# Two transformer layers on one core: weight blocks made behind each tile's sums, shared slots for the heads' large buffers, and every load on SP's queue

## The chip, the cores and the metric

The kernel runs on one core of one Trainium2 chip. The metric is the device time of one execution in microseconds (us). A core has TensorE (PE, with its weight loads as PEld), VectorE (DVE), ScalarE (ACT), GpSimd (POOL) and SyncE (SP). Each takes its own instructions in order, and they wait for one another, and for DMA transfers, through semaphores. A DMA is issued by one engine's instruction stream: in this kernel by SP or by ACT. Line numbers (L1091) are those of the kernel before.

## The reference

Two pre-norm layers, each of an attention and a feed-forward network (FFN), on x of 4 batches, 512 tokens and 1024 channels, in float32:

```python
x = x + L0_attention(layernorm(x))   # across the 4 batches, per token and channel group
x = x + L0_ffn(layernorm(x))         # base product + two of eight routed low-rank experts
x = x + L1_attention(layernorm(x))   # 32 causal heads, latent keys and values, rotary part
x = x + L1_ffn(layernorm(x))

def L1_attention(x):
    q = rmsnorm(x @ wq_a.T, q_a_ln_w) @ wq_b.T          # 256 -> 32 heads x (64 + 64)
    ckv, k_pe = split(x @ wkv_a.T)                      # 64 latent + 64 rotary channels
    kv = rmsnorm(ckv, kv_a_ln_w) @ wkv_b.T              # per head: 64 for keys, 128 for values
    scores = (q_full . k_full) * scale, causal
    return (softmax(scores) @ v) @ wo.T

def L1_ffn(x):
    routing = softmax(x[:, 179:-1].mean(1) @ router_W.T + router_b)     # per batch
    return x @ W.T + b + 2 * sum_e routing[e] * (x @ A[e].T) @ B[e].T
```

## The kernel before

The tokens are 16 tiles of 128 rows. Products are kept near float32 accuracy by splitting each operand into a high and a low part of type fp32r: ACT copies the high part (`ah`, `cxh`), and POOL or DVE subtracts it from the source for the low part (`al`, `cxl`). Three matmuls per product follow (`matmul3`, L133 to L135). A tile framework decides the order of the instructions on each engine from dependencies and from when buffers of its pools come free; an engine then runs that list strictly in order. SP's queue is one such list.

The stages, with their place in the profiled span:

- **Layer-0 attention**, up to about 107 us.
- **Layer-0 FFN**, to about 370 us, tile by tile: base products (`base`), routing, `finish`, statistics. Between its steps the loop advances a generator, `prepare_w1` (L366). It forms the differences of blocks of the last FFN's weights, `t1` to `t4` beside the plain `b11`, `b22`, `b21`, in halves s = 0 and 1. These go to DRAM (`w1_d`).
- **Projections of the layer-1 attention**, to about 468 us. They leave the queries' latents and the keys in DRAM.
- **Heads**, to 1560.8 us. 32 heads in four groups of eight; in a group, four batches; in a batch, eight units (one head each). A unit has scores and softmax (L773, L776), transposes of the probabilities (`turn`, L797), and the context product (`psv`, L813). `load_batch` (L563) fetches the next batch's latent queries `qT` (1.05 MB) and keys, double buffered. `prepare_output` (L888) builds the group's output weights from `wo` and `wv` (loaded by `fetch_output` into a pool of its own) as Strassen-like blocks b and t. Behind the next batch's units runs `project` (L820 on) as a filler: seven products per pair of tiles (`poa`, `pob`), added to rows `xs` of x that are loaded from `x_d` and stored again.
- **Transition and last FFN**, to the end. The last projection, of group 3 and batch 3, runs after the last unit, to 1602.6. The last FFN works on eight pairs of tiles q. `norm` and `turn1` (L1069) normalise and transpose a pair's blocks. `operands` (L1085 on) forms the seven combinations and splits them (L1090 ACT, L1091 POOL). `product` does seven steps for two halves of columns s, each 12 matmuls of 128x288. The first pair runs its seven steps with s = 0 first and then with s = 1. `biased` (L1191) adds the bias to the rows `xo` (and `raw`) on POOL, `mixture` makes the routing of a batch. The second pair starts at 1654.9.

The loads of that stage: `load_w1` issues them on ACT's queue, four t blocks of 1.18 MB and three b blocks of 0.59 MB for each s. s = 0 goes out once the attention's pools are closed (L1107), s = 1 once the projection has ended (L1138). `split_w1` splits the b blocks. `fetch_h` loads a pair's rows for `norm`, `fetch_x` loads them again as `xo`.

```python
def load_w1(kind, s):
    w = w1[kind, s] = w1p[s].tile([P, 2, ND // 2, W1B], FR, name=f"w{kind}{s}")
    if kind[0] == "t":
        nc.scalar.dma_start(out=f32(w), in_=w1_d[kind, s])
    else:
        nc.scalar.dma_start(out=f32(w)[:, 1], in_=w1_d[kind, s][:, 0])
```

Of the kernel before, what the change touches and what calls it, by code (L numbers as in the profile page):

```python
# [9 lines left out]
F32 = mybir.dt.float32  # L10
# [35 lines left out]
def block_kernel(ctx: ExitStack, tc: tile.TileContext, a: dict, out: bass.AP):  # L46
# [319 lines left out]
    def prepare_w1(room, u):  # L366

        c, s = divmod(u, 2)
        b11, b12, b21, b22 = (room[:, k * W1B : (k + 1) * W1B] for k in range(4))
        for n, (kind, to, a0, a1) in enumerate((("t1", b11, b12, b11), ("t3", b12, b22, b12),  # L370
                                                ("t2", b22, b22, b11), ("t4", b21, b21, b22))):
            V.tensor_tensor(to, a0, a1, ALU.subtract)
            n = 4 + 2 * ((4 * u + n) % 3)
            h, l = (room[:, (n + k) * W1B : (n + k + 1) * W1B].bitcast(FR) for k in range(2))
            A.copy(h, to)
            G.tensor_tensor(l, to, f32(h), ALU.subtract)
            nc.sync.dma_start(
                out=w1_d[kind, s][:, :, c, :],
                in_=room[:, n * W1B : (n + 2) * W1B].rearrange("p (k n) -> p k n", k=2))
            if kind == "t4" and u + 1 < ND:  # L380
                fetch_w1(room, u + 1)
            yield

    attn = ExitStack()
    cc = attn.enter_context(tc.tile_pool(name="c_const", bufs=1))
# [16 lines left out]
    with tc.tile_pool(name="b_h", bufs=2) as hp, tc.tile_pool(name="b_hTh", bufs=2) as hTh, \  # L402
# [64 lines left out]
        for s, t in enumerate(order):  # L467
            prep = prepare_w1(room1, s - 2) if 0 <= s - 2 < ND else iter(())
# [6 lines left out]
            next(prep, None)  # L475
# [7 lines left out]
            next(prep, None)  # L483
# [5 lines left out]
            next(prep, None)  # L489
# [11 lines left out]
            next(prep, None)  # L501
            if s == ND + 2:
                rawA = raw()
                for ch in range(ND):
                    nc.sync.dma_start(out=rawA[:, ch * NA : (ch + 1) * NA], in_=a["waT"][ch])
                split_shared(cc, 0)
# [6 lines left out]
    k_d = [dram.tile([P, TPB, KVR], F32, name=f"k_d{b}") for b in range(NB)]  # L513
    wqp = attn.enter_context(tc.tile_pool(name="c_wq", bufs=2))
# [48 lines left out]
    def load_batch(b):  # L563
        q = inp.tile([P, 2, 2, S], FR, name="qT")
        nc.sync.dma_start(out=f32(q), in_=q_d[b])
        kT = inp.tile([P, 2, S], FR, name="kT")
        nc.sync.dma_start(out=f32(kT), in_=kT_d[b])
        kF = inp.tile([P, P], F32, name="kF")
        nc.sync.dma_start(out=kF, in_=kF_d[b])
        k = inp.tile([P, TPB, KVR], F32, name="k")  # L570
        nc.sync.dma_start(out=k, in_=k_d[b])
        return q, kT, kF, k
# [38 lines left out]
    with tc.tile_pool(name="c1_w", bufs=1, side="right") as wap, \  # L611
# [73 lines left out]
        for s in range(NT + 1):  # L685
# [4 lines left out]
            if s > 0:  # L690
                keep(s - 1, qk[s - 1])
                if order1[s - 1] == TPB - 1:
                    batches[0, 0] = load_batch(0)
# [12 lines left out]

    with ExitStack() as c2:
# [6 lines left out]
        wop = heads.enter_context(tc.tile_pool(name="c2_wo", bufs=2))  # L714
# [165 lines left out]
        def fetch_output(g, pr):  # L880
            wo = [wop.tile([VD, D], F32, name="wo") for k in range(2)]
            for k in range(2):
                nc.sync.dma_start(out=wo[k], in_=a["woT"][g * HG + 2 * pr + k])
            wv = wop.tile([VD, 2, KVR], F32, name="wv")
# [79 lines left out]

        filler = None
        cx = behind = None
        for u in range(NU + 3):
# [38 lines left out]
            if u < NU:  # L1006
                g, b, i = units[u]
                if i == 2 and u + HG < NU:
                    nx = units[u + HG]
                    batches[nx[:2]] = load_batch(nx[1])  # L1010
                if b == 0 and i == 0:
                    wo_raw = fetch_output(g, 0)
                if (b, i) in ((NB - 1, 0), (NB - 1, 4)) and g + 1 < NG:
                    wq_raw = fetch_query(2 * g + 2 + i // 4)
        heads.close()
# [7 lines left out]
        w1p = [dp.enter_context(tc.tile_pool(name="d_w0", bufs=1))]  # L1023
# [5 lines left out]
        w1, hs, blocks, sums, stats, xo = {}, {}, {}, {}, {}, {}  # L1029
        late = raw()  # L1030

        def load_w1(kind, s):
            w = w1[kind, s] = w1p[s].tile([P, 2, ND // 2, W1B], FR, name=f"w{kind}{s}")
            if kind[0] == "t":
                nc.scalar.dma_start(out=f32(w), in_=w1_d[kind, s])
            else:
                nc.scalar.dma_start(out=f32(w)[:, 1], in_=w1_d[kind, s][:, 0])

        def split_w1(kind, s, eng):
            w = w1[kind, s]  # L1040
            A.copy(w[:, 0], f32(w)[:, 1])
            eng.tensor_tensor(w[:, 1], f32(w)[:, 1], f32(w)[:, 0], ALU.subtract)

        def load_x(q, tiles):
            for t in range(2):
                for k in range(2):
                    nc.sync.dma_start(out=tiles[t][:, k * 512 : (k + 1) * 512], in_=x_d[2 * q + t][k])
# [10 lines left out]
        def norm(q, t):  # L1058
            s = 2 * q + t
            normalise(hs[q][t], hs[q][t], *stats[s][0], stats[s][1])  # L1060
# [46 lines left out]
        fetch_h(0)  # L1107
        LOADS = ("b11", "b22", "b21", "t1", "t2", "t3", "t4")
        for kind in LOADS:
            load_w1(kind, 0)  # L1110
        mv = small.tile([P, TPB, 2], F32, name="mv")
# [7 lines left out]
        fetch_x(0)  # L1119
        advance(filler, 4)  # L1120
        for k in range(3):
            split_w1(LOADS[k], 0, G)
            advance(filler, 2)
            if k < 2:
                turn1(0, k)
            advance(filler, 2)
        fetch_h(1)
# [8 lines left out]
    lop = dp.enter_context(tc.tile_pool(name="d_lo", bufs=2, space=PSUM))  # L1136
    bias1 = broadcast_rows(w1r, a["b1"], D, "bias1")
    for kind in LOADS:  # L1138
        load_w1(kind, 1)
# [5 lines left out]
    nc.sync.dma_start(out=late[:, 0:D], in_=a["b1T"])  # L1145
# [81 lines left out]
    for q in range(NP):  # L1227
        inputs[q] = wk.tile([P, 2, ER], F32, name="inputs")
        odd, more = q % 2, q + 1 < NP
        if q == 0:  # L1230
            for step in range(7):
                product(0, step, (0,))
                if step > 3:
                    split_w1(LOADS[step - 4], 1, V)
        for step in range(7):
# [19 lines left out]
            if step == 4 and q == 0:  # L1255
# [92 lines left out]
```

## Time and profile before

| What | Value |
|---|---|
| runs shown | 1869.5, 1864.55, 1866.59 us; median 1866.59 |
| the profiled execution | 1862.94 us, its span 1861.0 us |
| mean granted TensorE clock | 0.982 |
| busy: PE, DVE, ACT, POOL | 1739.8, 1368.1, 875.0, 913.6 us |
| moved by DMA | 225.72 MB, mean 121 GB/s |
| SP's queue (q1), ACT's (q10) | 210.80 MB, 12.98 MB |

The page cuts the span into 40 slices of 46.5 us and gives each engine's busy share in tenths (9 is 90 % or more), the granted clock of TensorE and the DMA engines' share. A line of waits reads "engine, result and line <- what ended the wait: us in total, times, longest". A timeline row reads start, duration, engine, line, operation, result <- operands, count, and in brackets the idle time before it and what ended it. Rows such as ACTq or SPq are DMA issues on that engine. Busy shares mean different things in different stages: the stages above are bounded by different engines, so each is read by itself.

### The profile page before, as it was taken

How to read it: one execution, taken by the hardware profiler on the slowest of the kernel's cores; microseconds unless marked ns; L12 is line 12 of the kernel's file. 1: busy time of each engine (PE TensorE's matmuls, PEld its weight loads, DVE VectorE, ACT ScalarE, POOL GpSimd, SP SyncE). 2: the span in 40 equal slices, each digit the busy share in tenths (PEclk: the TensorE clock that was granted, in tenths of full speed). 3: DMA queues.
4: the chain of work that ended last, by engine and by line, in shares of the span. 5: the costliest groups of instructions: out<-in, count | busy, mean ns of one | idle time of the engine just before them, and what ended most of it. 6: DMA issues, size and time to landing. Idle time of an engine off the chain costs nothing.

```text
span 1861.0 us, 30786 instructions
## 1 busy us (share of the span) xinstructions
PE 1739.8 (93%) x10280; PEld 1461.4 (79%) x10280; DVE 1368.1 (74%) x3534; ACT 875.0 (47%) x2272; POOL 913.6 (49%) x819
## 2 busy tenths in 40 slices
PE   6978999999989999989999999999999998589998
PEld 6977899999667777757777757777757776488998
DVE  6787765576787777688777688777688875487685
ACT  6332211165665556465556465556465654233222
POOL 0364211010666666566666566666566653564552
PEclk9988999999999999999999999999999999799999
DMA  7235300034533324443324343324334326712431
GB/s 257 80 128 189 132 35 35 35 97 137 175 108 107 125 92 135 126 134 120 126 91 137 126 133 120 126 91 136 118 116 141 103 64 224 299 60 100 134 116 46
DMA packets 130813, 225.72 MB, mean 121 GB/s; under 512 B 22176, under 2 KB 58016, under 8 KB 127584
## 3 DMA queue, kind: packets, MB, share of 16 engines
q1 hardware_dynamic: 128640, 210.80, 34.4%
q10 hardware_dynamic: 2016, 12.98, 1.7%
q8 instruction: 81, 1.33, 0.3%
q14 instruction: 76, 0.62, 0.1%
HBM read 156.60 MB, written 70.65 MB: 122 GB/s over the span
## 4 chain that ended last, share of the span: by engine, by line
PE 70%; DVE 9%; POOL 4%; DMA 3%; ACT 3%; issue 2%; SPq 0%; POOLq 0%; ACTq 0%; DVEq 0%
PE psv L813 7%; PE pst L797 6%; PE pss L133 3%; PE pss L135 3%; PE pss L134 3%; PE po L133 3%; PE po L135 3%; PE po L134 3%; PE pob L133 3%; PE poa L133 3%; PE psq L133 3%; PE acc L135 3%; PE psq L135 2%; PE acc L133 2%; PE psq L134 2%; PE acc L134 2%
## 5 line engine op out<-in xcount | busy, mean ns | idle before, releaser
L776 ACT ACTIVATE p<-p,mn 128x512 f32<-128x512 f32 (+3 forms) x512 | 284.1, 557 | 240.3 <-DVE mn L773 239.6
L598 POOL TENSOR_TENSOR qf<-qf,ropeT 64x512 f32<-64x512 f32 x128 | 167.7, 1310 | 205.5 <-ACT qf L594 204.3
L773 DVE CUSTOM_DVE_ANT_0 p<-pss,causal 128x512 f32<-128x512 f32 (+3 forms) x512 | 231.7, 487 | 23.3 <-PE pss L135 19.5
L797 PE MATMUL pst<-ident,p 128*128 128x128 f32 x1280 | 185.4, 274 | 4.6 <-DVE pT L799 4.3
L599 POOL TENSOR_TENSOR qf<-qf,t 64x512 f32<-64x512 f32 x128 | 165.2, 1290 | 46.5 <-DVE t L597 39.0
L797 PEld LDWEIGHTS pst<-ident,p 128*128 128x128 f32 x1280 | 153.6, 142 | 32.9 <-DVE pT L799 7.4
L799 ACT COPY pT<-pst 128x512 f32<-128x512 f32 x256 | 143.7, 578 | 63.4 <-PE pst L797 63.4
L813 PE MATMUL psv<-pT,k 128*64 128x384 f32 (+3 forms) x1024 | 164.7, 441 | 0.0
L133 PE MATMUL pss<-kT,ql 128*128 128x512 f32 (+2 forms) x384 | 143.8, 374 | 22.0 <-POOL ql L607 13.9
L607 POOL TENSOR_TENSOR ql<-qf,qh 128x384 fp32r<-128x384 f32 x128 | 132.8, 1037 | 59.4 <-DVE qh L606 54.9
L835 POOL TENSOR_TENSOR cxl<-s,cxh 128x256 fp32r<-128x256 f32 x128 | 95.1, 744 | 131.3 <-ACT cxh L834 124.7
L133 PE MATMUL po<-w_h,hTl 128*128 128x384 f32 (+1 forms) x384 | 135.5, 353 | 13.3 <-DVE x L333 13.3
L813 PEld LDWEIGHTS psv<-pT,k 128*64 128x64 f32 x1024 | 73.2, 137 | 86.7 <-issue 75.8
L134 PE MATMUL po<-w_l,hTh 128*128 128x384 f32 (+1 forms) x384 | 132.1, 344 | 0.0
L135 PE MATMUL po<-w_h,hTh 128*128 128x384 f32 (+1 forms) x384 | 131.9, 344 | 0.0
L135 PE MATMUL pss<-kT,qh 128*128 128x512 f32 (+2 forms) x384 | 130.9, 341 | 0.0
L134 PE MATMUL pss<-kT,qh 128*128 128x512 f32 (+2 forms) x384 | 130.4, 340 | 0.0
L799 DVE COPY pT<-pst 128x256 f32<-128x256 f32 x128 | 53.9, 421 | 78.7 <-PE pst L797 77.1
L133 PEld LDWEIGHTS pss<-kT,ql 128*128 128x128 f32 x384 | 72.5, 189 | 45.0 <-POOL ql L607 18.1
L594 ACT COPY qf<-psq 128x512 f32<-128x512 f32 x126 | 73.9, 586 | 65.1 <-PE psq L135 62.8
L133 PE MATMUL psq<-qT,wql 128*128 128x512 f32 x252 | 101.7, 403 | 1.5 <-DVE t L597 1.5
L596 DVE TENSOR_TENSOR t<-psq,ropeT 32x512 f32<-32x512 f32 x126 | 87.7, 696 | 19.9 <-ACT qf L594 15.6
(521 smaller groups left out, 4975.7 us busy)
## 6 DMA issues: line engine op xcount, KB each, us to landing
xs<-x_d SPq DMA_DIRECT2D x128, 256.0 KB
x_d<-xs SPq DMA_DIRECT2D x128, 256.0 KB
qT<-q_d SPq DMA_DIRECT2D x16, 1024.0 KB
wo<-in_woT_dram SPq DMA_DIRECT2D x32, 512.0 KB
rb<-r_d SPq DMA_DIRECT2D x128, 128.0 KB
w_t<-raw SPq DMA_DIRECT2D x32, 288.0 KB
wt<-w_t ACTq DMA_DIRECT2D x8, 1152.0 KB
x<-in_x_dram SPq DMA_DIRECT2D x16, 512.0 KB
```

The lines of the kernel that those rows point to most:

```text
L133: T.matmul(ps, lhsT=al, rhs=bh, start=start, stop=False, **kw)
L134: T.matmul(ps, lhsT=ah, rhs=bl, start=False, stop=False, **kw)
L135: T.matmul(ps, lhsT=ah, rhs=bh, start=False, stop=stop, **kw)
L598: G.tensor_tensor(f[mid], f[mid], ropeT[mid, 0, :], ALU.mult)
L599: G.tensor_tensor(f[mid], f[mid], t2[mid], ALU.add)
L607: G.tensor_tensor(l, f[:, P:S], f32(h), ALU.subtract)
L773: V.tensor_tensor_reduce(out=to, in0=ps[:, 0:n], in1=causal[:, S - n : S], scale=1.0, scalar=-NEG, op0=ALU.add, op1=ALU.min, accum_out=mn[ ...
L776: A.activation(to, to, AF.Exp, bias=mn[:, i : i + 1], scale=-1.0, accum_out=rs[:, i : i + 1])
L797: T.transpose(ps[:, w : w + P], p[:, OF[i] + j * P : OF[i] + (j + 1) * P], ident)
L799: copy(pT[:, AT[js[0]] : AT[js[0]] + w], ps[:, 0:w])
L813: T.matmul(ps[n * KVR : (n + 1) * KVR, S - w : S], lhsT=k[:, j, :], rhs=pTs[u + n][:, AT[j] : AT[j] + w], start=(j == 0), stop=(j == TPB - 1))
L835: G.tensor_tensor(l, src, f32(h), ALU.subtract)
```

## The change

1. `prepare_w1` is a plain function. It is called once for each tile, after its `finish`, stores and statistics, and no longer a quarter at a time between the tile's products. The pool of the shared constants (`c_const`) opens after that stage.
2. Two slots, A and B, of 9216 bytes per partition each hold the latent queries and the keys of a batch, in turn by batch. A slot C holds one pair's `wo` and `wv`, in place of the pool `wop`. All three outlive the heads.
3. In the last batch of the last group the slots take weights of the last FFN: t1 into A (unit 4), t2 into C (unit 5), both s = 0. t3 later goes into B. The rows `xo` of the first pair and the transposed bias are asked for in unit 1 of that batch. The first pair is normalised from `xo[0]`, and `fetch_h(0)` is gone.
4. All loads of the weights go through SP's queue. The order of the loads for s = 1 is b11, b22, b21, t1, the bias, the router, t2, the second pair's rows, t3, t4.
5. `biased(0)` and the split of the transposed bias move from step 4 to step 6 of the first pair. The splits of b blocks alternate between POOL and DVE, and b21 of s = 0 is split after the first step.

The core of the diff:

```diff
@@ layer-0 FFN
-            prep = prepare_w1(room1, s - 2) if 0 <= s - 2 < ND else iter(())
...
-            next(prep, None)
+            if 0 <= s - 2 < ND:
+                prepare_w1(room1, s - 2)
@@ heads
+    slots = [ctx.enter_context(tc.tile_pool(name="slots", bufs=1))] * 2
...
+    def slot(k):
+        return slots[k].tile([P, ND * W1B], F32, name="slot" + "ABC"[k])
+
+    def load_batch(g, b):
+        room = slot((g * NB + b) % 2)
+        n = 4 * S
+        q = room[:, 0:n].bitcast(FR).rearrange("p (k c s) -> p k c s", k=2, c=2)
...
+        k = room[:, n : n + TPB * KVR].rearrange("p (j d) -> p j d", j=TPB)
...
         def fetch_output(g, pr):
-            wo = [wop.tile([VD, D], F32, name="wo") for k in range(2)]
+            room = slot(2)
+            wo = [room[:, k * D : (k + 1) * D] for k in range(2)]
...
+                if (g, b) == (NG - 1, NB - 1) and i == 1:
+                    late = raw()
+                    xo[0] = [late[:, (t + 1) * D : (t + 2) * D] for t in range(2)]
+                    load_x(0, xo[0])
+                    nc.sync.dma_start(out=late[:, 0:D], in_=a["b1T"])
+                if (g, b) == (NG - 1, NB - 1) and i in (4, 5):
+                    load_w1("t" + "12"[i - 4], 0, (0, 2)[i - 4])
@@ transition and last FFN
-                nc.scalar.dma_start(out=f32(w), in_=w1_d[kind, s])
+                nc.sync.dma_start(out=f32(w), in_=w1_d[kind, s])
...
-            normalise(hs[q][t], hs[q][t], *stats[s][0], stats[s][1])
+            normalise(hs[q][t], hs[q][t] if q else xo[0][t], *stats[s][0], stats[s][1])
...
-        fetch_h(0)
-        for kind in LOADS:
+        for kind in LOADS[:3]:
             load_w1(kind, 0)
...
-            split_w1(LOADS[k], 0, G)
+                split_w1(LOADS[k], 0, (G, V)[k])
...
+            if k:
+                load_w1("t" + "34"[k - 1], 0, (1, None)[k - 1])
...
-    for kind in LOADS:
-        load_w1(kind, 1)
+    for kind in LOADS[:4]:
+        load_w1(kind, 1)
...
+    load_w1("t2", 1)
+    fetch_h(1)
+    for kind in LOADS[5:]:
+        load_w1(kind, 1)
...
+                if step == 1:
+                    split_w1("b21", 0, G)
                 if step > 3:
-                    split_w1(LOADS[step - 4], 1, V)
+                    split_w1(LOADS[step - 4], 1, (V, G, V)[step - 4])
...
-            if step == 4 and q == 0:
+            if step == 6 and q == 0:
                 biased(0)
```

## The prediction

> **What bounds the kernel now.** I read the slices first, then the windows over the dip in them, the waits of that dip, and the timelines of PE, ACT and POOL.
>
> ```profile
> PE   6978999999989999989999999999999998589998
> PEclk9988999999999999999999999999999999799999
> DMA  7235300034533324443324343324334326712431
> PE 70%; DVE 9%; POOL 4%; DMA 3%; ACT 3%; issue 2%; SPq 0%; POOLq 0%; ACTq 0%; DVEq 0%
> ```
>
> PE is busy for 1739.8 of 1861.0 us, and is the bound nearly everywhere: what can be won is its gaps. After the start (layer 0) there is one dip, slices 33 to 35, from the end of the heads into the last FFN, and DMA is at its highest there (6, 7). By stage:
>
> ```profile
> 1535.00:1560.00 25.00, 24.98 (x149) 19.06 (x147) 15.71 (x44) 14.21 (x40) 10.29 (x12) 1.00 0.32 106
> 1560.00:1582.00 22.00, 14.76 (x67) 10.78 (x64) 10.40 (x16) 6.12 (x12) 7.42 (x9) 0.94 0.92 355
> 1582.00:1603.00 21.00, 17.38 (x71) 13.05 (x70) 18.09 (x22) 6.58 (x13) 17.49 (x14) 0.90 0.69 250
> 1603.00:1628.00 25.00, 5.47 (x42) 5.23 (x41) 1.90 (x6) 4.82 (x6) 6.34 (x5) 0.71 0.90 345
> 1628.00:1655.00 27.00, 22.11 (x141) 20.89 (x140) 21.37 (x28) 9.21 (x15) 21.20 (x14) 0.89 0.12 40
> ```
>
> The columns after the length are busy PE, weight loads, DVE, ACT, POOL, then granted clock, DMA share and GB/s. From 1603 to 1628 PE works 5.5 us and every compute engine is idle, with the DMA full: weights of the last FFN are awaited. The waits, and the rows in which they lie:
>
> ```profile
> PE acc L133 <- POOL al L1091: 22.0, 3, 19.5
> PE poa L133 <- POOL cxl L835: 4.4, 2, 4.1
> POOL xo L1191 <- DMA xo<-x_d: 18.7, 2, 14.4
> ACT ah L1090 <- issue: 17.2, 1, 17.2
> ```
> ```profile
> 1569.51 8.18 ACTq L1035 DMA_DIRECT2D wt<-w_t  x4
> 1577.79 0.40 ACT L834 CAST cxh<-s 128x256 fp32r<-128x256 f32 x1 [7.89 <-DMA wt<-w_t]
> 1609.24 5.12 ACTq L1035 DMA_DIRECT2D wt<-w_t  x4
> 1614.46 1.14 ACT L1090 CAST ah<-s 128x512 fp32r<-128x512 f32 x2 [17.22 <-issue]
> ```
> ```profile
> 1617.47 2.35 POOL L1191 TENSOR_TENSOR xo<-xo,bias 128x1024 f32<-128x1024 f32 x1 [14.37 <-DMA xo<-x_d]
> 1624.10 2.34 POOL L1191 TENSOR_TENSOR xo<-xo,bias 128x1024 f32<-128x1024 f32 x1 [4.29 <-DMA xo<-x_d]
> 1626.40 2.50 POOL L1091 TENSOR_TENSOR al<-s,ah 128x512 fp32r<-128x512 f32 x2
> ```
>
> PE's 19.5 us stall has three links: ACT issues weight loads and does no copies meanwhile; POOL stands before two bias adds whose xo arrives last in the same burst; the operand split al is behind them in POOL's queue. Earlier the same issuing on ACT delays cxh (7.89), hence cxl, hence the projection (4.1 of PE).
>
> **The change part by part.** Two landmarks of before: the last context matmul ends at 1560.8, the last output projection at 1602.6, and the second tile pair of the last FFN starts at 1654.9. So 41.8 us (A) and 52.3 us (B).
>
> *A after.* Work left on PE: 105 matmuls of 128x512 at 0.23 us start to start (21 of batch 2's last product, 84 of two pairs), 24.2; 16 transposes at 0.13, 2.1; the first 13 matmuls of the last FFN at 0.1325, 1.7. Sum 28.0. The change takes from this time the loads t1 and t2 (1.18 MB each, now issued in the last batch into the slots A and C, where windows show DMA at 0.32) and h(0) (1.05 MB, now normalised from xo): 3.4 MB, 8 us at 417 GB/s. ACT issues none. Left are the waits of before that had other causes (xs loads, POOL's order): before they were 1.9, 2.1, 1.0 and 0.5. I take 3.5 in all; bounds 1.5 and 9 (the 4.1 stall stays because t3, t4 and three b blocks still burst through SP ahead of xs). A = 31.5, projection end 1592.3.
>
> *B after.* Work: 155 matmuls at 0.1325, 20.5; 16 transposes, 2.1; sum 22.6. The two bias adds leave POOL's head (moved to step 6), so al comes first. The loads of s=1 still start only at the projection's end: 3 b blocks (0.59 MB), 4 t blocks, bias, xo and h of the second pair, 9.1 MB, 21.8 us at 417 GB/s. The first b block lands some 3 us in and is needed at 11.6 (after the s=0 half), t1 at 8.7 against 16, t4 at 18.2 against 21.2: margins of 2 us or more. POOL has some 12 splits of 1.3 to 1.8 and one weight split of 2.8: 21 of 25 us, a close second. I take 3 us of stalls; bounds 1 and 12. B = 25.6. The cold clock goes with the long stall (0.44 us per matmul against 0.29 until 1633.4).
>
> A and B give 94.1 - 57.1 = 37.0.
>
> *Bias adds, moved.* Four adds of 2.35 (9.4 us) now stand in a row on POOL between two al splits of the second pair's first steps. A step is 24 matmuls, 3.2 us, and al runs one to two steps ahead: 9.4 - 6.4 = 3 at most shows, part of it in place of the 2.2 us wait before: loss 1.5 (0 to 9.4).
>
> *Slots in the heads.* The slots A and B alternate by batch as the two buffers did, so the q loads stay over 32 us ahead; cost 0. Slot C holds wo and wv of one pair: in the compiled order the first block of outputs moves ahead of the first scores (470 us), with four ACT copies (0.58 each) before the Exp table load (1.28): loss 2.5 (-1 to +5; two later stalls of 0.9 and 1.7 may go). At the three later group starts the same preparations change places with scores: 0.5 each, 1.5 (-3 to +4). The cover is the 32 us per batch; without it a refill costs its own 2.6 us.
>
> *SP's queue.* Three b loads stand between the last unit's r_d store and rb load: rb comes 1.5 us later, with about 1.5 spare: 0.5 (0 to 2). t3 waits there for the last context matmul; behind it are the xs loads, not wanted before 1567.
>
> *Blocks behind the sums.* In the compiled order, layer 0 is unchanged on PE, DVE and ACT; on POOL a mask and three bias adds move ahead of a split with over 10 us of slack; on SP the rope table's load moves behind that stage: 0 (-1 to +1).
>
> *Two rules against it.* ACT spent 8.18 and 5.12 us issuing four loads, 2.0 and 1.3 each, where the data (1.18 MB) take 2.8. The Trainium skill, "DMA: Bandwidth & Descriptors", section "Issuing engines are not separate DMA queues", says that spreading issue over engines only saves sequencer time, usually small beside the transfer. By it the queue move is worth nothing, A keeps the 4.1 us and its cold clock of 2, and the sum is 6 less (1842). Here it is not small; I follow the row. Its section "Where 436 GB/s comes from" lets the HBM side bind at about 358 GB/s. The burst of 1609 to 1624 ran at 417, and 5 to 25 us, with SP's queue alone, at 407. At 358 the 9.1 MB take 25.4, the margins of t3 and t4 go and B grows by some 3.5. I follow the windows.
>
> **Sum.** 37.0 - 1.5 - 2.5 - 1.5 - 0.5 = 31.0. The profiled execution took 1862.94 (span 1861.0), so 1831.9; the median shown, 1866.59, lies 3.65 above it, which puts the change's median at 1835.6, said as 1836.
>
> **The rivals.**
>
> *The feed is the new bound* (0.22). B stays at 34 because al, weight splits and loads of s=1 all start at the projection's end and POOL has 21 us of them; A at 37. For: DVE 21.4 and POOL 21.2 busy in 1628:1655. Against: those 27 us included the recovery from the stall. Gain 18.3 + 4.8 - 6 = 17: 1850.
>
> *Better than forecast* (0.05): A and B fall to their work, 50.6, head costs vanish: gain 43, 1824.
>
> *The transition is mended and the heads eat it* (0.03), or the new order does not take hold because xo lands as late: 1863 to 1869.
>
> *Slower* (0.06): slot C. Twelve refills inside the groups can start only when the previous pair's matmuls are done, and they stand in SP's one queue, where a 1.05 MB q load (2.5 us) and a waiting store can be ahead. PE meets L901 in its order. For: one room instead of buffers; against: before, these loads held PE for 1.5 us in all (3 waits). Every refill late by 2.9 us (12 of them, 35) eats what the transition brings; late by 4 us each it is 48: 13 slower, 1880.
>
> **How the numbers follow.** The likeliest (0.64) is 1836, by itself 1828 to 1844. The range reaches into the feed rival: 1824 to 1856; outside are the no-change and slower cases (0.09), and the ends of the others (about 0.08). A difference under 0.3% (5.6 us) can't be told from none here. Faster 0.64 + 0.22 + 0.05 = 0.91, same 0.03, slower 0.06.
>
> **What would show it.** No ACTq weight loads; the wait of acc for al down from 19.5 to under 3; PE above 18 us of any 21 between 1560 and 1620, clock 0.95 or more; projection end near 1592 (+4 for the head start), second pair near 1618 (+4); four bias adds in a row on POOL after it. I am wrong if PE still waits over 6 us for al or a weight split in B (the feed), if xs waits stay 4 us (SP's queue), if L901 waits show up in the heads over 10 us in sum, or if the spacing of the 128 units changes.

## The result, and the profile after

The changed kernel takes **1851.3 us** (median of 5 runs, 1845.04 to 1854.41); the kernel before, run beside it, 1866.59 us (5 runs, 1863.86 to 1870.85). The ratio is **0.9909, 95 % interval 0.9883 to 0.9935**: faster by 0.9 %, with 1836 predicted. The profiled execution took 1851.48 us, span 1849.7.

The slices of the page of the kernel after, and its only large DMA queue:

```profile
PE   6978999999899999999999999999999999779998
...
PEclk9989899999899999999999999999999999989999
DMA  7235300035442333353243353242344233643431
...
q1 hardware_dynamic: 130080, 222.72, 35.9%
```

The dip has become shallower (7 and 7 in slices 34 and 35, where 33 to 35 had 8, 5 and 8), but it has not closed. ACT's DMA queue is gone from the list. The two stages of the prediction, A (last context matmul to the end of the projection) and B (from there to the second pair), are cut exactly in the windows of both kernels; before first, then after. The columns are those of the prediction's windows.

```profile
1560.80:1602.80 42.00, 31.14 (x127) 23.19 (x126) 28.30 (x36) 12.70 (x25) 24.81 (x21) 0.92 0.83 311
1602.80:1654.90 52.10, 27.68 (x182) 26.22 (x181) 23.36 (x34) 14.02 (x21) 27.54 (x18) 0.80 0.49 187
```
```profile
1567.10:1605.50 38.40, 31.22 (x137) 24.04 (x136) 28.35 (x38) 11.48 (x24) 21.51 (x20) 0.96 0.63 212
1605.50:1642.50 37.00, 28.05 (x175) 26.48 (x174) 21.06 (x37) 13.78 (x20) 20.81 (x15) 0.86 0.68 263
```

A fell from 42.0 to 38.4 and B from 52.1 to 37.0, where 31.5 and 25.6 were predicted. The DMA is no longer the limit in A (0.63 busy). PE's waits after, in 1450 to 1720 us, and the rows of B in which they lie:

```profile
PE acc L133 <- DVE raw L1244: 6.5, 2, 3.3
PE pob L133 <- DVE xs L877: 5.3, 3, 2.4
...
PE acc L133 <- POOL al L1110: 1.2, 2, 0.9
```
```profile
1612.69 0.61 PE L133 MATMUL acc<-wb,al 128*128 128x288 f32 x1 [3.23 <-DVE raw L1244]
...
1633.56 0.58 PE L133 MATMUL acc<-wb,al 128*128 128x288 f32 x1 [3.26 <-DVE raw L1244]
```

The 19.5 us wait for POOL's `al` is gone. What PE waits for now is the emptying of a product's accumulator (`acc`) into `raw` and `inputs` by DVE. DVE's own list shows why that is late:

```profile
1606.71 1.23 DVE L1282 TENSOR_TENSOR b1l<-raw,b1h 128x1024 fp32r<-128x1024 f32 x1 [0.46 <-ACT b1h L1281]
1609.12 0.69 DVE L1103 TENSOR_TENSOR s<-a,a 128x512 f32<-128x512 f32 x1 [1.18 <-POOL al L1110]
1609.84 1.64 DVE L1103 TENSOR_TENSOR s<-s,a 128x512 f32<-128x512 f32 x1
1611.52 0.69 DVE L1103 TENSOR_TENSOR s<-a,s 128x512 f32<-128x512 f32 x1
1612.12 0.28 DVE L1240 COPY inputs<-acc 128x128 f32<-128x128 f32 x1
```

PE's second product ended at 1608.6, and its transposes at 1609.5. But `inputs<-acc` stands in DVE's list behind the split of the transposed bias (`b1l`) and three operand sums `s` of the first pair's second pass. The first of those sums waits for POOL. In these rows no data are missing: the instruction that frees PE's accumulator is queued behind others. (A second wait lies hidden behind these sums; a_ol below brings it out.) The second stall, at 1633.56, is the same with a `sum` that had waited 5.0 us for ACT:

```profile
1631.20 0.69 DVE L1095 TENSOR_REDUCE sum<-pt 128x4 f32<-128x512 f32 x1 [5.00 <-ACT a L1090]
```

### The profile page after: what moved, and what is told of

It reads as the page before. It is cut to its first block, busy times and chain, and to the rows that moved or that the text cites. A ratio compares the mean times of both kernels' runs of the same rounds, so it can differ in the third digit from the quotient of the medians.

```text
span 1849.7 us, 30780 instructions
## 1 busy us (share of the span) xinstructions
PE 1744.4 (94%) x10280; PEld 1463.2 (79%) x10280; DVE 1363.8 (74%) x3534; ACT 878.0 (47%) x2272; POOL 915.7 (50%) x819
## 3 DMA queue, kind: packets, MB, share of 16 engines
q1 hardware_dynamic: 130080, 222.72, 35.9%
## 4 chain that ended last, share of the span: by engine, by line
PE 70%; DVE 10%; POOL 4%; ACT 3%; issue 2%; DMA 1%; SPq 0%; POOLq 0%; ACTq 0%; DVEq 0%
PE psv L817 8%; PE pst L801 6%; PE pss L133 3%; PE pss L134 3%; PE pss L135 3%; PE pob L133 3%; PE poa L133 3%; PE po L133 3%; PE po L134 3%; PE po L135 3%; PE psq L133 3%; PE acc L135 3%; PE acc L133 2%; PE pob L134 2%; PE psq L135 2%; PE pob L135 2%
## 5 line engine op out<-in xcount | busy, mean ns | idle before, releaser
L133 PE MATMUL pss<-kT,ql 128*128 128x512 f32 (+2 forms) x384 | 144.4, 376 | 19.8 <-DVE mn L777 14.4
L839 POOL TENSOR_TENSOR cxl<-s,cxh 128x256 fp32r<-128x256 f32 x128 | 96.7, 756 | 116.9 <-ACT cxh L838 111.6
L133 PE MATMUL po<-w_h,hTl 128*128 128x384 f32 (+1 forms) x384 | 136.0, 354 | 13.4 <-DVE x L333 13.4
L600 DVE TENSOR_TENSOR t<-psq,ropeT 32x512 f32<-32x512 f32 x126 | 87.7, 696 | 17.2 <-ACT qf L598 13.0
L780 ACT ACTIVATION_READ_ACCUMULATOR p<-p,mn 128x1 f32 x512 | 96.3, 188 | 0.0
L479 POOL TENSOR_TENSOR x<-x,bias 128x1024 f32<-128x1024 f32 x16 | 38.9, 2431 | 106.1 <-DVE h L124 82.3
L601 DVE TENSOR_TENSOR t<-psq,ropeT 32x512 f32<-32x512 f32 x126 | 87.1, 691 | 1.7
```

Of the source, the lines that this page charges most:

```text
L133: T.matmul(ps, lhsT=al, rhs=bh, start=start, stop=False, **kw)
L780: A.activation(to, to, AF.Exp, bias=mn[:, i : i + 1], scale=-1.0, accum_out=rs[:, i : i + 1])
L839: G.tensor_tensor(l, src, f32(h), ALU.subtract)
```

## The experiments

Times are medians, ratios are to the kernel before on the same chip, and A, B and "pair 2" (second to third pair's start) come from each profile, one execution per kernel. "Rest" is the span of that profile from the projections' first transposes (`pn<-ident,qn`) to its end, so all but layer 0 and the first of the projections. "First pass" and "second pass" mean the seven steps of the first pair with s = 0 and with s = 1.

| Kernel | us | ratio, 95 % interval | A | B | pair 2 | rest |
|---|---|---|---|---|---|---|
| before | 1866.59 | | 41.9 | 52.1 | 33.7 | 1473.3 |
| after | 1851.3 | 0.9909, 0.9883 to 0.9935 | 38.4 | 37.0 | 36.1 | 1460.4 |
| b_sp | 1853.45 | 0.9930, 0.9915 to 0.9945 | 47.4 | 32.3 | 38.7 | 1463.0 |
| a_act | 1871.56 | 1.0026, 1.0012 to 1.0040 | 41.6 | 56.7 | 36.0 | 1483.4 |
| b_bias | 1864.87 | 0.9993, 0.9981 to 1.0004 | 42.4 | 49.8 | 37.1 | 1476.1 |
| b_gen | 1864.76 | 0.9982, 0.9965 to 0.9999 | 42.4 | 52.6 | 35.3 | 1477.9 |
| a_wop | 1851.36 | 0.9896, 0.9857 to 0.9935 | 37.2 | 36.0 | 44.6 | 1462.4 |
| a_ol | 1844.29 | 0.9885, 0.9848 to 0.9923 | 36.9 | 37.8 | 33.9 | 1459.4 |
| a_wkh | 1850.58 | 0.9902, 0.9870 to 0.9934 | 38.3 | 35.9 | 36.2 | 1462.2 |
| a_fix3 | 1844.02 | 0.9875, 0.9846 to 0.9904 | 38.4 | 35.1 | 37.0 | 1459.2 |
| a_fix3wop | 1849.73 | 0.9899, 0.9872 to 0.9925 | 38.7 | 33.2 | 45.0 | 1457.9 |
| a_fix5 | 1854.55 | 0.9928, 0.9911 to 0.9946 | 38.4 | 37.1 | 38.9 | 1465.2 |
| a_fix5v | 1854.05 | 0.9921, 0.9900 to 0.9943 | 38.4 | 31.1 | 42.0 | 1460.8 |
| a_fix3v | 1846.39 | 0.9892, 0.9870 to 0.9915 | 36.9 | 32.1 | 39.9 | 1456.4 |

Those transposes begin anywhere from 383.4 to 391.4 us in these profiles, also between kernels that have the same code up to there (after 389.3, a_ol 385.4, a_fix3 383.7). A median that differs by a few us is therefore held against "rest" before the edit is credited with it. After is 12.9 us below before in it, b_sp 10.3.

### Which part carries the gain: the queue alone, and everything but the queue

b_sp is the kernel before with its weight loads on SP's queue, and nothing else. a_act is the kernel after with those loads on ACT's.

```diff
 # b_sp
-                nc.scalar.dma_start(out=f32(w), in_=w1_d[kind, s])
+                nc.sync.dma_start(out=f32(w), in_=w1_d[kind, s])
...
-                nc.scalar.dma_start(out=f32(w)[:, 1], in_=w1_d[kind, s][:, 0])
+                nc.sync.dma_start(out=f32(w)[:, 1], in_=w1_d[kind, s][:, 0])
 # a_act: the same two lines of the kernel after, the other way round
```

> The kernel before with one part of the change alone: its 14 weight loads are issued by SP instead of ACT. Theory 1 (the queue is the cause: ACT's copies stood behind the issues, and with them al, cxl and the place of the two xo bias adds on POOL): the projection ends 5 to 8 us sooner after the last context matmul (41.9 before), the 19.5 us wait of acc falls below 8, in all 13 to 22 us faster. Theory 2 (the rule that the issuing engine only saves sequencer time, with bytes and bias order as the cause): within 4 us of before, and the long wait of acc stays over 15.

> The changed kernel with its weight loads put back on ACT's queue; slots, early loads and everything else stay. If the queue carries most of the gain, 8 to 18 us slower than the changed kernel, with ACT issue rows of several us in the transition and a wait of acc or of the projection behind them. If bytes taken out of the burst carry it, 0 to 5 us slower.

b_sp has 0.70 % of the 0.91 %; the two intervals overlap, so the rest of the change is not told apart from nothing by these two runs. Of its first theory the total holds (13.4 us below the runs of before beside it) and so does the wait of acc (6.3, under 8). A does not: it grew by 5.5 us where it should have shrunk by 5 to 8. In a_act the early loads and the slots are all there, and it is 0.3 % slower than before and about 20 us behind after, a little more than the 8 to 18 expected. PE's waits, its ACT row and POOL's rows in a_act:

```profile
PE acc L133 <- POOL al L1110: 23.3, 1, 23.3
```
```profile
1610.93 5.84 ACTq L981 DMA_DIRECT2D wt<-w_t  x4
1616.87 1.14 ACT L1109 CAST ah<-s 128x512 fp32r<-128x512 f32 x2 [15.88 <-DMA rb<-in_rb_dram]
```
```profile
1623.98 2.34 POOL L1213 TENSOR_TENSOR xo<-xo,bias 128x1024 f32<-128x1024 f32 x1 [18.59 <-DMA xo<-x_d]
...
1632.21 2.49 POOL L1110 TENSOR_TENSOR al<-s,ah 128x512 fp32r<-128x512 f32 x2
```

With the loads on ACT, `ah` comes at 1616.9, and on POOL the two `xo` bias adds stand ahead of `al`, as before. In b_sp the order on POOL is another: an `al` is at 1619.95, and the two `xo` adds follow at 1645.08, after all splits of the first pair.

```profile
1619.95 2.23 POOL L1091 TENSOR_TENSOR al<-a,ah 128x512 fp32r<-128x512 f32 x1 [9.79 <-ACT ah L1090]
...
1645.08 5.58 POOL L1191 TENSOR_TENSOR xo<-xo,bias 128x1024 f32<-128x1024 f32 x2
```

So the one edit works twice: ACT is free to copy, and the order that the framework gives POOL changes with it (why, was not followed). No run separates the two. The rows of before in the prediction allow an estimate: two `ah` were done by 1615.6 and the first `al` began at 1626.40, so some 11 us of the 19.5 lay behind the two adds alone.

*What held ACT.* The prediction took ACT's rows of 8.18 and 5.12 us for issuing, 2.0 and 1.3 us a load. But such a row merges four instructions with the time between them. One by one they take 0.33 to 0.45 us (least, median and most, in ns, in the kernel before):

```profile
L1035 ACTq DMA_DIRECT2D wt<-w_t x8: 326/326/445, 1569.5 to 1613.9; - x8
```

The first four start at 1569.51, 1571.87, 1576.07 and 1577.36. By the trace's semaphores, ACT stood before the last three until an earlier transfer had landed: a b load at 1571.85, a store of `xs` at 1576.05, and the first of the four themselves at 1577.34. So ACT did not spend its time on issuing. It waited for transfers at the head of its list, with the copies behind.

On SP's queue, in b_sp, the four loads go out in 3.44 us, and it is loads of `xs` that come late behind them. PE's waits of b_sp show those rows in the second line:

```profile
1573.70 3.44 SPq L1035 DMA_DIRECT2D wt<-w_t  x4
...
1583.49 11.09 SPq L845 DMA_DIRECT2D xs<-x_d  x4
```
```profile
PE acc L133 <- POOL al L1091: 9.4, 3, 6.3
PE pob L133 <- DVE xs L873: 5.4, 2, 4.2
```

That is part of why A is longer in b_sp (47.4 against 41.9). The 6.3 us wait for `al` also lies in it, and so do matmuls of the last FFN that stood in B before (161 matmuls in A against 127). A and B together are 79.7 us, against 94.0 before.

### Whose bias adds stood at POOL's head

The prediction laid the two adds to `biased(0)`, which the change moves from step 4 to step 6. b_bias makes that move alone.

```diff
-            if step == 4 and q == 0:
+            if step == 6 and q == 0:
                 biased(0)
```

> The kernel before with biased(0) and the split of the transposed bias moved from step 4 to step 6, nothing else. The recorded prediction took these to be the two adds at the head of POOL's queue: then the 19.5 us wait of acc loses 6 to 16 us. Rival: the two adds on xo that al stood behind belong to the second pair (they write xo, the first pair's write raw), which this step does not move: then the wait stays at 17 to 21 and the time within 3 us.

Nothing moved: PE still waits 19.3 us, and POOL's list has the same two adds at the head.

```profile
PE acc L133 <- POOL al L1091: 19.3, 1, 19.3
```
```profile
1623.50 2.35 POOL L1191 TENSOR_TENSOR xo<-xo,bias 128x1024 f32<-128x1024 f32 x1 [14.35 <-DMA xo<-x_d]
1629.90 2.34 POOL L1191 TENSOR_TENSOR xo<-xo,bias 128x1024 f32<-128x1024 f32 x1 [4.05 <-DMA xo<-x_d]
```

All four adds of the first two pairs have one line, L1191. In this list the first pair's rows are in `raw` and the second pair's in `xo`: the two at the head are `biased(1)`, hoisted there. The name of the result says whose rows they are; the line does not.

### The blocks behind the sums, alone

b_gen makes part 1 of the change in the kernel before.

```diff
-            prep = prepare_w1(room1, s - 2) if 0 <= s - 2 < ND else iter(())
...
-            next(prep, None)
+            if 0 <= s - 2 < ND:
+                prepare_w1(room1, s - 2)
```

> The kernel before with part 1 of the change alone: the weight blocks made once behind each tile's sums, the pool of shared constants opened later. The prediction put this at 0 (within 1 us); the instruction order of PE, DVE and ACT in layer 0 is that of before. The time at which the projections' transposes begin was 387.7 to 390.6 us in three profiles of kernels with the old layer 0 and 383.7 to 389.5 in seven with the new one, so the rival is a gain of 2 to 3 us from POOL's or SP's order. 0: ratio within 0.1 %; the rival: 0.12 to 0.2 % faster.

The ratio is 0.9982 (0.9965 to 0.9999), at the edge of what can be told. It has the size that the rival expected, but no stage of its profile is clearly shorter, and the projections' transposes begin later in it (390.5) than before (387.7). Over the fourteen profiles they begin at 383.4 to 391.4 us, at 387.7 to 390.6 in those with the old order of part 1. Effects of 2 us cannot be placed there.

### What slot C is worth

a_wop gives `wo` and `wv` their own pool again, and loads t2 in the transition. a_fix3wop does the same to a_fix3 (below).

```diff
-    slots.append(ctx.enter_context(tc.tile_pool(name="slotC", bufs=1, side="right")))
...
+        wop = heads.enter_context(tc.tile_pool(name="c2_wo", bufs=2))
...
-        for kind in LOADS[:3]:
+        for kind in LOADS[:3] + ("t2",):
```

> The changed kernel without slot C: wo and wv go back to a pool of the heads, and t2 of s=0 is loaded with the b blocks at the transition. Theory (slot C takes back what it brings): the head start and the group starts lose nothing against before (4.7 us by the last unit with slot C, 0 to 1 here), while the projection and the time to the second pair grow by 0 to 4 us for 1.18 MB more in the burst: 1 to 5 us faster than the changed kernel. Rival (the heads' loss has another cause, for instance slots A and B or SP's order): the 4.7 us stay and it is 0 to 4 us slower.

> Both: no slot C, inputs off the stores, and the sums held. By the sum of the parts, 5 to 11 us faster than the changed kernel (1840 to 1846 in the median); if the later t2 eats what the holds bring, within 3 us of a_wop.

Without slot C the time is the same, 1851.36 against 1851.3. It was expected 1 to 5 us faster. The heads are 4.1 us shorter, as its theory had it: 2.6 from the projections' first transposes to the exponentials of unit 8 (counted from 0), 1.5 from there to the last context matmul. A and B, which were to grow, are shorter too. But pair 2 grows from 36.1 to 44.6. Its PE rows:

```profile
1641.17 0.57 PE L1180 MATMUL pt<-each,ones 128*128 128x8 f32 x2 [4.33 <-DVE each L1178]
1648.64 0.45 PE L318 MATMUL pt<-ident,hw 128*128 128x128 f32 x1 [2.78 <-issue]
```

The second pair starts 8 us earlier on the clock than after, and then waits for the routing of the batch (`each`, then `hw`). That routing needs sums of both pairs' rows and passes through DVE's list. The same holds for a_fix3wop: B 33.2, pair 2 45.0, and 1849.7 where the sum of the parts gave 1840 to 1846. So slot C is neutral in the median. It costs 4 us in the heads and brings 6 from the last context matmul to the third pair (111.5 against 117.8 without it). That the early t2 does this was not shown: the memory layout changes with slot C too, and the path from t2 to the late routing was not followed.

### The order of DVE's list in B

Three edits, alone and together. a_ol holds three operand sums of the second pass behind emptyings of the accumulator (steps 2, 3, 4 of the first pass). It also held the first load of `wo` behind an exponential, without effect: SP issued the load at 442.1, and ACT's first exponential is at 478.1. a_wkh opens the pool of `inputs` earlier, so that `inputs` no longer lies over `xs`, and holds ACT's copy of the transposed bias, meant to wait for step 2 of the second pass. That hold, too, stands between two engines: the split `b1l` runs at 1611.96, still in the first pass, but no longer ahead of the first emptyings (in a_fix3 at 1608.09). a_fix3 has all of a_wkh and the holds of the sums, behind steps 3, 4 and 5.

```diff
 # a_ol; in a_fix3 held(3), held(4), held(5)
+            for turn_, q in enumerate((0, *range(NP))):
+                def held(step):
+                    return tc.issue_after(evac[step].ins) if turn_ == 1 else ExitStack()
...
+                with held(2):
+                    s1 = add("s1", a21, a22, ALU.add)
 # a_wkh and a_fix3: this line stands before the pool d_w1 is opened, no longer behind it
+    wk = dp.enter_context(tc.tile_pool(name="d_work", bufs=2, side="right"))
```

> The changed kernel with two holds. (1) the operand sums of the second pass over the first pair wait for the evacuations of steps 2, 3 and 4 (they stood ahead of them on DVE, waiting for POOL's al, while PE waited 3.2 us for a bank): that wait and its 1.3 us of half clock go, 37.0 us from the projection's end to the second pair become 31 to 34; if instead al or the weight splits are what is late, the same 3 us show up as a wait of acc for POOL. (2) the first wo load is held until the first unit's last exponential: the head start's loss (2.9 us at the fifth unit) shrinks to under 1. Together 4 to 8 us faster than the changed kernel; 0 to 2 if the waits only move.

> The changed kernel with one pool in another place: the rows inputs, written by DVE when it evacuates t1 and t2, no longer lie over the buffers xs of the last projection, so that they don't wait for its last stores; the split of the transposed bias, which does lie there, is held until step 2 of the second pass. If that wait is one of the two in line behind PE's 3.2 us at b22, the 37.0 us from the projection's end to the second pair become 32 to 35. If the operand sums standing before the evacuations are the only cause, it stays at 36 to 38.

> The same, and the operand sums of the second pass held behind the evacuations of steps 3, 4 and 5. If the two waits stand in line (each hides the other), only now does the stretch become 30 to 33, and the time 4 to 7 us less than the changed kernel's; the 3.3 us wait five steps later (a sum over transposed rows behind POOL's al) should stay. If POOL's or ACT's throughput is the bound, 36 to 38 stays and waits for al take over.

In a_ol the sums are out of the way, and B is no shorter (37.8). The emptying now stands first, and waits for something else:

```profile
1607.46 0.29 DVE L1250 COPY inputs<-acc 128x128 f32<-128x128 f32 x1 [3.00 <-DMA x_d<-xs]
```
```profile
1608.03 0.40 PE L133 MATMUL acc<-wb,al 128*128 128x288 f32 x1 [2.04 <-DVE raw L1254]
```

`inputs` lies over `xs`, and the last stores of `xs` must land first. Two waits stood one behind the other, and each hid the other. In the kernel before the second was there too, under the 19.5 us stall:

```profile
DVE inputs L1218 <- DMA x_d<-xs: 7.0, 1, 7.0
```

a_wkh takes away the second, with `b1l`, and gives 1 us in B, within the runs' spread (35.9; 32 to 35 expected if it counted, 36 to 38 if not). a_fix3 takes away both. DVE then stands idle before the same emptying and waits only for PE's product, and PE now waits for POOL:

```profile
1600.79 0.29 DVE L1247 COPY inputs<-acc 128x128 f32<-128x128 f32 x1 [0.77 <-PE acc L135]
```
```profile
PE acc L133 <- POOL al L1111: 7.8, 4, 3.0
```

So B has a third wait behind the first two: 35.1 with both mended, where 30 to 33 was expected. a_fix3 (1844.0) and a_ol (1844.3) have the lowest medians of all kernels here, 7 us below after, about as much as was expected of them. But their intervals overlap with its, and the profiles don't support the holds as the cause. In "rest" they are only 1.2 and 1.0 us below after. Most of what their profiles are shorter by lies in layer 0 (5.6 and 3.9 us), whose code is the same. Behind it a_ol gains 1.5 us in A and 2.2 in pair 2, and loses 0.8 in B, where it was aimed, and 2.0 in the heads.

### The heads' start, and DVE beside POOL

a_fix5 has the early pool, the holds of a_ol, a hold on the split `b1l`, and a hold of the first matmuls of output blocks behind unit 1's last score matmul. a_fix5v and a_fix3v let DVE make the low parts `al` of the second pass, in a_fix5 and in a_fix3.

```diff
 # a_fix5
+                    with tc.issue_after(lastmm[1].ins) if g == 0 and n == 0 else ExitStack():
+                        T.matmul(po[k * KVR : (k + 1) * KVR, :], lhsT=wv[:, k, :],
+                                 rhs=wo[k][:, half * 512 : half * 512 + 512], start=True, stop=True)
 # a_fix5v, a_fix3v
-                G.tensor_tensor(l, src, f32(h), ALU.subtract)
+                (V if turn_ == 1 else G).tensor_tensor(l, src, f32(h), ALU.subtract)
```

> The changed kernel with inputs off the stores, the operand sums of the second pass held behind the evacuations of steps 2, 3 and 4, the split of the transposed bias held behind step 4 of the second pass, and PE's matmuls for the first output block held behind the second unit's scores, so that DVE takes the first scores before the subtraction t10. If the head start's loss is that subtraction standing 3.9 us before the first scores, the eighth unit comes 2 us or more sooner after the start of the transposes' stage (149.3 us in the changed kernel, 146.9 before). From the last context matmul to the third pair: 106 to 109 us (111.5 in the changed kernel). Together 4 to 8 us under the changed kernel, 1843 to 1847 in the median. If the waits only move again, within 3 us.

> The same, but the low parts al of the second pass over the first pair are made by DVE and not by POOL. Theory (in this stretch DVE's subtractions with two inputs in SBUF wait for POOL's instruction to end): the sums s of 128x512 take 0.7 us here, where they took 1.6 to 2.9 beside POOL, and the stretch gets shorter by 0 to 4 us although DVE has seven subtractions more. Rival (they are slow for another reason, such as the DMA burst): the sums stay at 1.6 to 2.9, and the stretch gets longer by 3 to 8 us.

> The version with both mended orders (blocks of the second pass not over xs; operand sums of the second pass held behind the evacuations of steps 3, 4, 5), and in addition the operand splits al of that second pass made by DVE in place of POOL. Theory (POOL's al is what PE still waits for, and DVE's two-input adds are slow only while POOL runs): PE's waits for POOL al (7.8 us in the version without this edit) go to under 3, the stage from the projection's end to the second pair's start falls from 35.1 to about 29, the adds s of that stage take 0.7 us each, and if the second pair keeps its 37 us the time is about 1838 (from 1844.0). Rival (the work only moves: DVE enters the second pair later, with the same evacuations and bias adds to do): the stage is shorter by the same 6 us, but the second pair lengthens by 3 to 6 us, as it did (38.9 to 42.0) when this edit was made with the other holds, and the time stays at 1842 to 1846. Second rival (DVE becomes the late one): the stage stays at 35 or more, with waits for DVE al in place of POOL al, and the time is 1846 or more.

*The start.* In the kernel after, the first scores are computed at 470.85, and their first result `p` is made 8.1 us later (1.1 us later in the kernel before, at 470.18 after 469.11). In the row before it DVE waits for a block of outputs:

```profile
478.32 0.69 DVE L917 TENSOR_TENSOR raw<-raw 128x512 f32<-128x512 f32 x1 [3.88 <-POOL b110l L921]
478.93 0.68 DVE L777 CUSTOM_DVE_ANT_0 p<-pss,causal 128x512 f32<-128x512 f32 x1
```

If that were the cause, a_fix5 would remove it. It does move the blocks, and the first `p` comes 7.7 us after the first scores all the same (472.69 to 480.39), since its buffer waits for a store of the stage before; PE stands 6.9 us:

```profile
480.39 0.69 DVE L779 CUSTOM_DVE_ANT_0 p<-pss,causal 128x512 f32<-128x512 f32 x1 [4.11 <-DMA kT_d<-kT]
```
```profile
481.14 0.58 PE L133 MATMUL pss<-kT,ql 128*128 128x256 f32 x1 [6.90 <-DVE mn L779]
```

Again two waits in line. So a_fix5 missed what it was for: unit 8 was to come 2 us sooner and came 1.5 later, the stretch from the last context matmul to the third pair is 114.4 us (106 to 109 expected, 111.5 after), and the median is 1854.6, not 1843 to 1847. Its profile is also its slowest run (1858.96). In a_wop, without slot C, the first `p` comes 1.1 us after the scores, as in the kernel before. So the cost comes with slot C. That it comes from what `p` then lies over in memory is a reading of the row above: a layout that keeps slot C and moves `p` was not tried.

*DVE beside POOL.* The same two sums of B, in a_fix5 with POOL making `al`, and in a_fix5v, where the first of them starts 0.1 us ahead of POOL's next instruction (1615.96) and the second lies in POOL's idle time (1619.1 to 1635.2):

```profile
1615.37 1.34 DVE L1107 TENSOR_TENSOR s<-s,a 128x512 f32<-128x512 f32 x1
...
1623.32 1.75 DVE L1107 TENSOR_TENSOR s<-a,a 128x512 f32<-128x512 f32 x1 [0.79 <-POOL al L1114]
```
```profile
1615.86 0.68 DVE L1107 TENSOR_TENSOR s<-s,a 128x512 f32<-128x512 f32 x1
...
1623.36 0.68 DVE L1107 TENSOR_TENSOR s<-a,a 128x512 f32<-128x512 f32 x1
```

In the second kernel the sums take 0.68 us, as the theory had it. B falls from 37.1 to 31.1, and pair 2 grows from 38.9 to 42.0. a_fix3v shows the same with the other holds: B from 35.1 to 32.1 and pair 2 from 37.0 to 39.9. The waits for POOL's `al` fall from 7.8 to 2.1, but 4.2 for DVE's `al` take part of their place. The time does not fall in either (1854.05 against 1854.55; 1846.39 against 1844.02). The first rival of the last expectation holds in the main: the work moves. From the last context matmul to the third pair a_fix3v has 108.9 us against 110.5 in a_fix3, less than the runs' spread, and a_fix5v 111.6 against 114.4 in a_fix5.

## Why the prediction was right or wrong, point by point

**The sum of the profiles.** The span fell by 11.3 us. A and B gave 18.7 of the 37.0 predicted. The last context matmul came 6.3 us later (1567.13 against 1560.86; 1.6 of it in layer 0). Pair 2 took 2.4 more, and what follows it 1.3 less: 18.7 - 6.3 - 2.4 + 1.3 = 11.3. The medians differ by 15.3; the profiled execution of before was 3.65 below its median. So the change brought half of the 31 us forecast. The measured 1851.3 lies outside the 1828 to 1844 of the likeliest case, and inside the stated range only because that was stretched to the feed rival, whose cause holds only in part (below). That is luck.

**What was right.**
- The bound (PE's gaps around the transition), the first link (ACT issuing loads) and the vanishing of the 19.5 us wait. The move to SP's queue, which the rule of the Trainium skill ("DMA: Bandwidth & Descriptors", "Issuing engines are not separate DMA queues") would price at next to nothing, is worth 13 us by itself in b_sp, more than twice the 6 taken. What the section says of the issue itself agrees with the trace: 0.33 to 0.45 us each, beside some 2.8 us for the data. The 13 us come from what an issue waited for in ACT's list, and from POOL's order, so "here it is not small" was right in the total and wrong in its reading of the rows.
- The head start (2.5): 2.3 up to unit 8. The mechanism, copies and blocks ahead of the first scores, was one of two waits in line; moving the blocks alone (a_fix5) brought nothing.
- Group starts (1.5): 1.8, and 0.6 more inside the first group.
- Four bias adds in a row (1.5): POOL's list has them from 1641.71 to 1652.06, and pair 2 is 2.4 longer. The late `hw` (waits of 1.75 and 2.02) has its part in that.
- The slower rival was rightly held small: slot C costs some 4 us in the heads and not 48.
- Of the signs named, there are no ACTq loads, the wait for `al` is 1.2, and no waits at the output blocks' line add up to 10 us. The projection's end (1605.5 against 1592 + 4), the second pair (1642.5 against 1618 + 4) and B's clock (0.86 against 0.95) missed. The waits for `xs` add up to 6.0 (the longest 2.45).

**What was wrong.**
- *"I take 3 us of stalls; bounds 1 and 12"* in B. It was 37.0 against 22.6 of work: 14.4, above the upper bound. PE's waits are 3.23, 0.97, 0.30, 0.29, 3.26 and 0.91, in sum 9.0. Behind the two long ones 12 and 24 matmuls run at the cold clock, 3.0 us and 5.9 us where 0.1325 each would be 1.6 and 3.2: 4.1 more. That leaves 1.3 unplaced. The sum asked when the loads land and how much POOL has to do. It did not ask what stands in DVE's list ahead of each emptying of the accumulator. The wait before (19.5 us) had given DVE time to do all of it unseen, the 7.0 us that `inputs` waited for `x_d<-xs` included.
- *"I take 3.5 in all; bounds 1.5 and 9"* in A. The waits are 2.45, 2.09, 0.62, 0.79 and 1.23 us, 7.2; A took 10.4 over its 28.0 of work, above the upper bound. Behind the first wait the clock is half from 1578.4 to 1581.4, and seven matmuls of 128x512 there take 0.43 us each where 0.23 was counted, 1.4 more; 1.8 are unplaced. Four of these five are for DVE's sum into `xs`. DVE has one weight split of 1.88 us more in its list there, and two-input adds that are held up beside POOL's splits. The loads were not the limit over the stage: DMA was 0.63 busy.
- *"The two bias adds leave POOL's head (moved to step 6)"*. They were those of the second pair; moving `biased(0)` does nothing (b_bias). The head of POOL's list came clear with the loads' move to SP, as b_sp and a_act show. The wait vanished as forecast, for a wrong reason: luck.
- The feed rival came near in the time (1850), in A (37) and in B (34), and only in part in the cause. It held POOL's 21 us of splits for the bound. POOL is busy 20.8 of the 37.0, and PE's long waits are for DVE. But with those mended PE waits 7.8 us for POOL (a_fix3), and taking `al` from POOL shortens B by 6.0 and 3.0 us (a_fix5v, a_fix3v), though not the kernel. B's waits chain through the lists of DVE, POOL and ACT; no run shows one engine as its bound.

**Where the early loads went.** b_sp, without them, is 2 us behind after. From the last context matmul to the third pair they save 6.9 us (111.5 against 118.4). Slot C's 4 us in the heads take more than half of that, and what is left is within the spread of runs.

**Open.** What part 1 does (0.9982 with an interval that just misses 1); why the medians of a_ol and a_fix3 are 7 us lower, with layer 0 shorter and the rest not; why the queue of the loads changes POOL's order; and which buffer `p` shares with the stores at the heads' start.

## What to carry to other kernels

When a long stall goes, list what every engine had been doing under its cover. On each engine that frees or fills the next operand, read which instructions stand ahead of the one that matters, and price those, not only bandwidth and busy time. Waits often stand in line: mend one alone and nothing moves, and the trace names only the last to end. When a compute engine issues loads, look at each issue by itself: a short instruction that waits for an earlier transfer holds all that stands behind it. Moving the issue may also reorder a third engine's list; try that edit alone before building anything bigger on it. And compare two profiles first in the stages that the edit does not touch.

## What the runs showed of the hardware

- **Two-input adds on DVE beside POOL.** An add of 128x512 from two SBUF operands takes 0.68 us alone and up to 2.9 us when it comes while POOL runs. In A, an add of 128x256 (0.43 alone) took 2.29, ending with POOL's split:

```profile
1572.25 2.29 DVE L832 TENSOR_TENSOR s<-s,cx 128x256 f32<-128x256 f32 x1
...
1581.01 0.43 DVE L832 TENSOR_TENSOR s<-s,cx 128x256 f32<-128x256 f32 x1
```
```profile
1571.04 3.22 POOL L988 TENSOR_TENSOR wb<-wb 128x1152 fp32r<-128x1152 f32 x1 [0.32 <-ACT wb L987]
```

  POOL's split ran to 1574.26 and the add to 1574.54, 0.28 later. The Trainium skill, "SBUF — State Buffer", section "SBUF: two separate sides", describes this as an exclusive lock: whichever starts first, a DVE operation with two SBUF inputs or a GpSimd operation that reads SBUF, keeps the shared ports to its end. The rows agree. Emptyings that read the accumulator kept their 0.44 us beside POOL in B.
- **The length of a wait does not tell whether the clock halves.** After the two waits of 3.2 us in B, matmuls of 128x288 took 0.44 us in place of 0.29, for 3.0 and 5.9 us, so that the stalls cost 4.6 and 6.0 in all. The half clock also followed waits of 1.79 us (at 765.57) and 2.45 us (at 1577.09), but not one of 2.09 (at 1586.53), and in a_wkh not one of 3.11 (at 1631.51). The third column from the end is the granted clock, of after and then of a_wkh:

```profile
765.57:770.00 4.43, 4.43 (x19) 4.10 (x20) 2.44 (x9) 3.63 (x11) 2.59 (x4) 0.61 0.42 133
1577.09:1581.50 4.41, 4.41 (x13) 3.34 (x14) 2.01 (x6) 1.33 (x3) 2.66 (x3) 0.63 0.77 261
1586.53:1591.00 4.47, 3.85 (x16) 2.90 (x17) 4.47 (x6) 1.96 (x4) 3.19 (x3) 1.00 0.25 91
1612.69:1615.90 3.21, 3.21 (x14) 3.21 (x15) 1.64 (x3) 0.93 (x1) 2.21 (x1) 0.52 1.01 423
1633.56:1639.70 6.14, 6.10 (x24) 5.75 (x24) 3.14 (x8) 0.71 (x3) 0.69 (x1) 0.50 0.01 3
```
```profile
1631.51:1638.00 6.49, 4.81 (x34) 4.58 (x35) 4.48 (x11) 1.24 (x2) 2.92 (x3) 1.00 0.01 3
```
- **A DMA issue is short, and can hold its engine's list for long.** The eight t loads on ACT took 0.33 to 0.45 us each as instructions. The first four went out over 8.18 us, with ACT waiting between them for earlier transfers to land.
